# A two-layer decoder on one core: activations grouped by their table, and the end of a running maximum taken in single chunks

## The chip, the core and the metric

The kernel runs on one core of a Trainium2 chip. TensorE (PE in the profile) multiplies matrices, VectorE (DVE), ScalarE (ACT) and GpSimd (POOL) work element by element, and SyncE (SP) issues the transfers. Each engine takes its own instructions in order. The metric is device time in microseconds; lower is better. All data is float32.

## The reference, cut to what matters

The input is 32 sequences of 56 tokens with 128 features, and for each sequence a context of 1500 rows of 128 features. Six blocks follow one another, each added to its input and layer-normalised:

```python
x = _layernorm(x + _L0_attn_ref(x, ...), axis=-1)               # windowed self-attention, 16 heads
x = _layernorm(x + _L0_xattn_ref(ctx_1024, ctx_1024, x, ...))   # one-head attention to the context
x = _layernorm(x + _L0_ffn_ref(x, w_up, w_down, ...))           # 8 experts of 512 units, gelu, top 2 of a softmax router
x = _layernorm(x + _L1_attn_ref(x, ...))                        # recurrent mixer
x = _layernorm(x + _L1_xattn_ref(x, ctx_1024, ...))             # 16 heads of 64 attend to the context
x = _layernorm(x + _L1_ffn_ref(x, ...))                         # shared expert and 8 experts of 256 units, top 2
```

The change touches the third block (layer 0's experts, and the two weights of the chosen experts, which are a softmax over the two largest router logits) and the fifth (layer 1's attention to the context: scores, softmax over 1500 rows, and the weighted sum).

## The kernel before, in words

**Layer 1's attention** (`attention`, L1041) is the backbone. The projections of query and key are folded into one 128x128 matrix for each head, so a sequence has 16 x 56 = 896 query columns. They are cut into two blocks, 512 and 384 columns wide; 32 sequences give 64 blocks. For a block, 12 matmuls make the scores `s` of 12 chunks of 125 context rows (through 3 banks of the pool `p_s`); ScalarE copies each chunk to SBUF (L1065); VectorE keeps a running maximum `m`, two chunks at a time, after chunks 3, 5, 7, 9 and 11 (L1068), and at the end folds its two halves into one (L1076). TensorE then transposes `m` (`maxima`, tile `t<-ident,m`), VectorE reduces it to the negative maximum of each query, and TensorE spreads that back (`spread`). Only then, in a second pass over the scores, VectorE adds the negative maximum (L1150) and ScalarE takes the exponential (L1153), three chunks at a time, in four parts (`probabilities`). The first of these parts run between the value matmuls of the block before, the rest (`tail`) in the score phase of the block after. The value matmuls of a block (`values`, 12 for each tile of 128 queries, tile `v`) come one block later, between the scores of the next block and those of the one after: so TensorE has 12 value matmuls between a block's last scores and the transposes of its maximum. The results are transposed into `qo` by `outputs` (L1173, tile `t<-ident,ao`), called at chunk 9 of a later score phase.

**Everything else** is filler: generators that the attention loop advances between its own pieces. `pre(g)` runs layer 0 and the mixer for a group of four sequences (`self_attention`, `cross_attention_0`, `experts_0`, `recurrent_mixer`, `queries_1`), `post(k)` runs layer 1's output projection and experts. A `Thread` holds a generator; `until(th, us)` steps it while its TensorE time, counted by the planner's own estimate, is under what is due. Each `yield` gives a delay that the planner lets pass before the next step. When the attention reaches a group whose `pre` isn't through, `finish` runs the rest at once, with little beside it. The first two groups run before the attention begins: a `leader` and a `follower`, stepped in turn. The framework that builds the program then orders the instructions once more by priority, readiness and free buffers, so the program's order is not exactly the order of the calls.

**`experts_0`** (L703) makes the router's logits, picks two experts (`top2`), and computes the two weights `p1`, `p2` with an exponential on ScalarE (L723), an addition, a reciprocal and a product on VectorE, and from them `wmix` (`mix`). Then, for each of 8 experts, four units of 128: a matmul into a bank of the pool `p_f` (two banks, tag `f`, shared by all filler) and a gelu on ScalarE (L740), with a `yield 0` after each; then the down-projection of the expert before (`down`) and its weighted addition to `acc` (L757). Behind the first expert's gelus, TensorE transposes `wmix` and VectorE copies it to `wT` (L751), from which the experts' biases are added (`bdn`). The weights of the next expert are issued on SP's queue at the start of each expert.

**Tables.** ScalarE needs the right activation table for a function. The builder puts a load (`ACT_TABLE_LOAD` in the profile, `LoadActFuncSet` in the program) wherever the next function isn't in the active table. Gelu and the exponential are in different tables; tanh, copy and identity need no load beside either. In the profile, a load carries the line of the activation behind it.

Of the kernel before, what the change touches and what calls it, by code (L numbers as in the profile page):

```python
# [10 lines left out]
AF = mybir.ActivationFunctionType  # L11
ALU = mybir.AluOpType
AX = mybir.AxisListType

B, S, D, SK = 32, 56, 128, 1500
# [13 lines left out]
PK, CK = 125, 12  # L29
# [40 lines left out]
def decoder_kernel(  # L70
# [35 lines left out]
    def bank(pool, tag):  # L106
        if pool is p_f and place["aside"]:
            pool, tag = p_s, "s"
        return pool.tile([P, 512], F32, tag=tag, name=tag)
# [36 lines left out]
    def mm(ps, lhsT, rhs, start=True, stop=True):  # L146
        nc.tensor.matmul(ps, lhsT=lhsT, rhs=rhs, start=start, stop=stop)  # L147
        n = math.prod(rhs.shape[1:])

        k, m = lhsT.shape[0], math.prod(lhsT.shape[1:])  # L150
        part = 0.5 if k <= 32 else 0.25 if m <= 32 else 0.5 if m <= 64 else 1.0
        clock["pe"] += part * max(4 * n * CYCLE + 0.016, MATMUL_MIN)
# [175 lines left out]
    def linear(lhsT, rhs, n, m=P):  # L328
        ps = bank(p_f, "f")
        mm(ps[:m, :n], lhsT, rhs)  # L330
        return ps[:m, :n]
# [71 lines left out]

    def self_attention(xs):
# [294 lines left out]
    def experts_0(xs):  # L703
        nj, nt = len(xs), len(xs) * TP
        nu = U0 // D

        def weights(e):
            wu = wst.tile([P, U0], F32, tag="w0", name="wu0", bufs=4)
            nc.sync.dma_start(wu, wup0[:, e * U0 : (e + 1) * U0])
            wd = wst.tile([P, U0], F32, tag="w0", name="wd0", bufs=4)  # L710
            nc.sync.dma_start(wd, wdn0[:, e * U0 : (e + 1) * U0])
            return wu, wd

        ws = weights(0)
        xT = to_features(xs, "xT")
        yield HOP
        lg = tiny.tile([TP, nj, E], F32, tag="lg", name="lg", bufs=2)
        nc.vector.tensor_copy(lg, router(xT, C_R0, nj))
        picks = top2(lg)
        p1 = tiny.tile([TP, nj], F32, tag="p1", name="p1", bufs=2)  # L720
        p2 = tiny.tile([TP, nj], F32, tag="p2", name="p2", bufs=2)
        nc.vector.tensor_tensor(p2, picks[1][0], picks[0][0], ALU.subtract)
        nc.scalar.activation(p2, p2, AF.Exp)  # L723
        nc.vector.tensor_scalar_add(p1, p2, 1.0)
        nc.vector.reciprocal(p1, p1)
        nc.vector.tensor_tensor(p2, p2, p1, ALU.mult)
        w = mix(picks, (p1, p2))
        yield 0
        acc = []
        hT = None  # L730
        for e in range(E + 1):
            last = (ws, hT)
            if e < E:
                if e > 0:
                    ws = nxt
                if e + 1 < E:
                    nxt = weights(e + 1)
                hT = hidden_tile()[:, :, :nt]
                for u in range(nu):
                    nc.scalar.activation(  # L740
                        hT[:, u, :], linear(ws[0][:, u * D : (u + 1) * D], xT, nt), AF.Gelu,
                        bias=vec[:, C_BUP + e * nu + u : C_BUP + e * nu + u + 1],
                    )
                    yield 0
            if e == 0:

                wT = work.tile([E, T], F32, tag="wT", name="wT", bufs=1)[:, :nt]
                ps = bank(p_f, "f")
                for j in range(nj):
                    tr(pair(ps[:E], j), w[:, j, :])  # L750
                nc.vector.tensor_copy(wT, ps[:E, :nt])  # L751
                yield HOP
                for j in range(nj):
                    acc.append(plus(linear(pair(wT, j), bdn, D, TP), xs[j], "acc"))
            else:
                for j in range(nj):
                    nc.vector.scalar_tensor_tensor(  # L757
                        acc[j], down(last[1], last[0][1], nu, j),
                        w[:, j, e - 1 : e], acc[j], ALU.mult, ALU.add,
                    )  # L760
                    yield 0
        return acc


# [281 lines left out]
    def attention():  # L1046
        blocks = [(b, q0, n) for b in range(B) for q0, n in BLOCKS]
        prev = None
        old = None
        tail = []  # L1050
        for i in range(len(blocks) + 2):
            cur = None
            if i < len(blocks):
                b, q0, n = blocks[i]
                if q0 == 0:
                    if b % 2 == 0 and any(b // 2 == pairs[0] for pairs in GROUPS):
                        yield ("need", b // 2)
                s = sbig.tile([P, CK, n], F32, tag=f"s{n}", name=f"s{n}")[:PK]
                m = mid.tile([P, 2, 512], F32, tag="m", name="m")[:PK, :, :n]
                qT = qo[(b // 2) % 3][:, b % 2, q0 : q0 + n]  # L1060
                cur = (b, q0, n, s)
                for c in range(CK):
                    ps = bank(p_s, "s")
                    mm(ps[:PK, :n], amT[:, c * PK : (c + 1) * PK], qT)
                    nc.scalar.copy(s[:, c, :], ps[:PK, :n])  # L1065
                    if c % 2 == 1 and c > 1:
                        a = s[:, 0:2, :] if c == 3 else m
                        nc.vector.tensor_tensor(m, a, s[:, c - 1 : c + 1, :], ALU.max)  # L1068
                    if c % 2 == 0 and tail:
                        tail.pop(0)()  # L1070
                    if c == 9 and old is not None:
                        outputs(old)
                        old = None
                    if c % 2:
                        yield 0
                nc.vector.tensor_tensor(m[:, 0, :], m[:, 0, :], m[:, 1, :], ALU.max)  # L1076
                if q0 and b + 1 < B:
                    load_attended_T(b + 1)
            elif old is not None:
                outputs(old)  # L1080
                old = None
            for f in tail:
                f()
            tail = []
            os = []
            nt = prev[2] // P if prev else 0
            for t in range(max(nt, 2)):
                if t < nt:
                    po = values(prev, t)
                    for k in range(3):  # L1090
                        next(po)
                        if t == 1 and k == 1 and cur:
                            nb = spread(cur, nm)
                            tail = probabilities(cur, nb)
                            for f in tail[:1]:
                                f()
                            tail = tail[1:]
                        yield 0
                    os.append(next(po))
                elif t == 1 and cur:  # L1100
                    yield 1.0
                    nb = spread(cur, nm)
                    tail = probabilities(cur, nb)
                if t == 0 and cur:
                    if not nt:
                        yield 1.0
                    nm = maxima(cur, m)
                if t >= 2 and tail:
                    tail.pop(0)()
            if prev:  # L1110
                old = (prev, os)
            if cur and cur[1] == 0 and cur[0] + 1 < B:
                load_attended(cur[0] + 1)
            prev = cur
# [20 lines left out]
    def spread(blk, nm):  # L1135

        n = blk[2]
        ps = bank(p_t, "t")
        for t in range(n // P):
            tr(ps[:PK, t * P : (t + 1) * P], nm[:, t : t + 1].to_broadcast([P, PK]))  # L1140
        nb = mid.tile([PK, 512], F32, tag="nb", name="nb")[:, :n]
        nc.scalar.copy(nb, ps[:PK, :n])  # L1142
        return nb
# [39 lines left out]
    class Thread:  # L1183
        def __init__(self, gen, aside=None):
            self.gen, self.spent, self.at, self.over = gen, 0.0, 0.0, False
            self.aside = aside

        def step(self):
            t0 = clock["pe"]
            place["aside"] = self.aside  # L1190
            try:
                lat = next(self.gen)
            except StopIteration:
                lat, self.over = 0, True
            place["aside"] = None
            self.spent += clock["pe"] - t0
            self.at = clock["pe"] + (lat or 0)
            return lat is not None

        def drain(self, *others):  # L1200
# [39 lines left out]

    def until(th, us):
        while not th.over and th.at <= clock["pe"] and th.spent < us:
            if not th.step():
                break

# [125 lines left out]
```

## Time and profile before

| | |
|---|---|
| time, median of 3 runs | 2231.57 us (2231.19 to 2233.58) |
| the profiled execution | 2235.22 us, its span 2233.5 us |
| mean granted TensorE clock | 0.988 |
| busy: PE, DVE, ACT, POOL | 2160.7, 1434.5, 1269.0, 139.4 us |
| activation-table loads on ACT | 43 at L740, 34 at L1153, 9 at L723, 1 at L268, each 1283 ns |

Each engine's row gives the time in which it had an instruction running. For TensorE, the end of a matmul is modelled, so 97% busy doesn't mean that it runs at its peak. The waits say whom an engine waited for, and a wait is only worth something if it lies on the way to the end. The granted clock is a share of TensorE's full speed over a stretch of time.

### The profile page before, as it was taken

How to read it: one execution, taken by the hardware profiler on the slowest of the kernel's cores; microseconds unless marked ns; L12 is line 12 of the kernel's file. 1: busy time of each engine (PE TensorE's matmuls, PEld its weight loads, DVE VectorE, ACT ScalarE, POOL GpSimd, SP SyncE). 2: the span in 40 equal slices, each digit the busy share in tenths (PEclk: the TensorE clock that was granted, in tenths of full speed). 3: DMA queues.
4: the chain of work that ended last, by engine and by line, in shares of the span. 5: the costliest groups of instructions: out<-in, count | busy, mean ns of one | idle time of the engine just before them, and what ended most of it. 6: DMA issues, size and time to landing. Idle time of an engine off the chain costs nothing.

```text
span 2233.5 us, 36792 instructions
## 1 busy us (share of the span) xinstructions
PE 2160.7 (97%) x14560; PEld 1709.6 (77%) x14560; DVE 1434.5 (64%) x2926; ACT 1269.0 (57%) x2207; POOL 139.4 (6%) x230
## 2 busy tenths in 40 slices
PE   7899999999999999999999999999999999999997
PEld 5667778678877888777877778777887778778787
DVE  4368554776567656766567665776557766676674
ACT  2555575566655566555665466656565556565551
POOL 2000001100010000100001000110001000000000
PEclk9899999999999999999999999999999999999999
DMA  7621322043211432025311243114330132111221
GB/s 198 173 85 31 111 51 94 17 125 85 93 30 56 117 86 79 22 68 127 94 55 31 77 114 105 48 29 111 92 98 28 56 103 74 51 40 44 66 80 37
DMA packets 164299, 172.16 MB, mean 77 GB/s; under 512 B 9464, under 2 KB 136864, under 8 KB 164000
## 3 DMA queue, kind: packets, MB, share of 16 engines
q1 hardware_dynamic: 164128, 169.82, 27.0%
q8 instruction: 115, 1.88, 0.4%
q14 instruction: 56, 0.46, 0.1%
HBM read 144.29 MB, written 25.49 MB: 76 GB/s over the span
## 4 chain that ended last, share of the span: by engine, by line
PE 80%; DVE 9%; ACT 5%; POOL 2%; DMA 2%; issue 1%; SPq 0%; POOLq 0%; ACTq 0%; DVEq 0%
PE f L147 29%; PE s L147 24%; PE v L147 21%; PE f L156 4%; PE t L156 3%; DVE s L1150 3%; ACT s L1153 2%; POOL rs L360 2%; DVE m L1068 2%; DMA memT<-big 1%; DVE st L351 1%; DMA wu<-in_wup_dram 0%; ACT nb L1142 0%; ACT s L1065 0%; DVE y L365 0%
## 5 line engine op out<-in xcount | busy, mean ns | idle before, releaser
L147 PE MATMUL v<-amN,s 125*128 125x129 f32 x5376 | 702.2, 276 | 2.6 <-ACT s L1153 1.8
L147 PEld LDWEIGHTS v<-amN,s 125*128 125x128 f32 x5376 | 662.4, 192 | 39.6 <-issue 22.3
L147 PE MATMUL s<-qo,amT 128*125 128x512 f32 (+1 forms) x1536 | 652.3, 544 | 2.4 <-ACT s L1065 2.2
L1065 ACT COPY s<-s 125x512 f32<-125x512 f32 (+1 forms) x768 | 399.2, 537 | 211.0 <-PE s L147 206.4
L1150 DVE TENSOR_TENSOR s<-s,nb 125x1536 f32<-125x1536 f32 (+1 forms) x256 | 393.2, 1549 | 63.2 <-ACT nb L1142 62.8
L147 PEld LDWEIGHTS s<-qo,amT 128*125 128x125 f32 x1536 | 264.4, 188 | 162.0 <-issue 93.3
L1153 ACT ACTIVATE s<-s 125x1536 f32<-125x1536 f32 (+1 forms) x256 | 339.1, 1328 | 85.5 <-DVE s L1150 79.3
L1068 DVE TENSOR_TENSOR m<-m,s 125x1024 f32<-125x1024 f32 (+1 forms) x256 | 278.5, 1088 | 78.8 <-ACT s L1065 75.3
L360 POOL TENSOR_TENSOR rs<-rs,mhalf 112x1 f32<-112x1 f32 x126 | 81.7, 660 | 1721.3 <-DVE rs L359 1465.1
L1170 ACT ACTIVATE ao<-v,rz 128x128 f32<-128x128 f32 x224 | 80.9, 364 | 152.9 <-DVE rz L1168 152.5
L740 ACT ACTIVATE hT<-f,vec 128x224 f32<-128x224 f32 (+1 forms) x256 | 106.3, 437 | 106.2 <-PE f L147 104.1
L147 PE MATMUL f<-xT,wu 128*128 128x224 f32 (+1 forms) x512 | 135.2, 368 | 4.9 <-DMA wu<-in_wup_dram 3.1
L147 PEld LDWEIGHTS f<-wd,hT 128*112 128x112 f32 x960 | 115.3, 180 | 15.5 <-ACT hT L740 4.5
L147 PE MATMUL f<-wd,hT 128*112 128x128 f32 x960 | 125.2, 279 | 1.2 <-ACT hT L740 1.2
L147 PE MATMUL f<-pxT,w 128*128 128x224 f32 (+1 forms) x576 | 118.0, 344 | 2.0 <-DVE th L923 0.7
L147 PEld LDWEIGHTS f<-pxT,w 128*128 128x128 f32 x576 | 98.5, 194 | 17.8 <-DVE th L923 3.7
L147 PEld LDWEIGHTS f<-xT,wu 128*128 128x128 f32 x512 | 86.9, 199 | 32.8 <-ACT hT L740 10.4
L1068 DVE TENSOR_TENSOR m<-s 125x1024 f32<-125x1024 f32 x64 | 69.5, 1086 | 55.0 <-ACT s L1065 54.7
L1142 ACT COPY nb<-t 125x512 f32<-125x512 f32 x64 | 34.0, 531 | 113.5 <-PE t L156 113.2
L757 DVE SCALAR_TENSOR_TENSOR acc<-f,wmix,acc 112x128 f32<-112x128 f32 x120 | 41.5, 348 | 85.0 <-PE f L147 85.0
L147 PE MATMUL f<-w,h 128*112 128x128 f32 x512 | 79.9, 279 | 1.9 <-DVE th L923 1.9
L147 PEld LDWEIGHTS f<-w,h 128*112 128x112 f32 x512 | 66.7, 177 | 17.7 <-issue 4.5
(291 smaller groups left out, 2366.1 us busy)
## 6 DMA issues: line engine op xcount, KB each, us to landing
amT<-memT SPq DMA_DIRECT2D x32, 750.0 KB
amN<-in_mem_dram SPq DMA_DIRECT2D x34, 672.0 KB
memT<-big SPq DMA_DIRECT2D x30, 750.0 KB
cxN<-in_mem_dram SPq DMA_DIRECT2D x30, 672.0 KB
wu<-in_wup_dram SPq DMA_DIRECT2D x72, 256.0 KB
wd<-in_wdn_dram SPq DMA_DIRECT2D x72, 256.0 KB
w<-in_gate_dram SPq DMA_DIRECT2D x72, 128.0 KB
w<-in_up_dram SPq DMA_DIRECT2D x72, 128.0 KB
```

What stands on the lines that cost most here:

```text
L147: nc.tensor.matmul(ps, lhsT=lhsT, rhs=rhs, start=start, stop=stop)
L156: nc.tensor.transpose(ps, in_, ident[:k, :k])
L351: nc.vector.bn_stats(st, r)
L360: nc.gpsimd.tensor_tensor(rs, rs, mhalf[:TP], ALU.pow)
L740: nc.scalar.activation(hT[:, u, :], linear(ws[0][:, u * D : (u + 1) * D], xT, nt), AF.Gelu, bias=vec[:, C_BUP + e * nu + u : C_BUP + e * n ...
L757: nc.vector.scalar_tensor_tensor(acc[j], down(last[1], last[0][1], nu, j), w[:, j, e - 1 : e], acc[j], ALU.mult, ALU.add,)
L1065: nc.scalar.copy(s[:, c, :], ps[:PK, :n])
L1068: nc.vector.tensor_tensor(m, a, s[:, c - 1 : c + 1, :], ALU.max)
L1142: nc.scalar.copy(nb, ps[:PK, :n])
L1150: nc.vector.tensor_tensor(c, c, nb.unsqueeze(1).to_broadcast([PK, 3, n]), ALU.add)
L1153: nc.scalar.activation(c, c, AF.Exp)
L1170: nc.scalar.activation(o, po[:, :D], AF.Copy, scale=rz)
```

## The change

Four things are done.

- In `experts_0`, gelus come in pairs: two units' matmuls go into the two halves of one bank, and two gelus read it. In front of each pair the generator yields a marked delay, `Gelu(0)`. A flag `table["gelu"]` is cleared when the attention begins a block's exponentials and set again when its `tail` is empty, in the next block's score phase. While the flag is clear, `until` holds a thread that stands before a pair of gelus, unless the thread is within 5 us of what is due to it, or past it.
- The router's two weights are made with tanh in place of the exponential: `0.5 + 0.5 tanh(d/2)` and `0.5 - 0.5 tanh(d/2)`, one ScalarE and two VectorE instructions. The transposition of `wmix` and the biases move from behind expert 0's gelus to behind expert 1's. The `yield 0` of the down-projections stands ahead of each instead of behind it.
- The running maximum: the chunks 3, 5, 7 and 9 still go two at a time; right after chunk 9's, the two halves are folded into one; then chunks 10 and 11 are taken singly, each as soon as it is copied. The fold at the end is gone.
- `outputs` is called at chunk 5 instead of chunk 9.

```diff
+    class Gelu(float):
+        pass
+    table = {"gelu": True}
...
-        nc.scalar.activation(p2, p2, AF.Exp)
-        nc.vector.tensor_scalar_add(p1, p2, 1.0)
-        nc.vector.reciprocal(p1, p1)
-        nc.vector.tensor_tensor(p2, p2, p1, ALU.mult)
+        nc.scalar.activation(p2, p2, AF.Tanh, scale=0.5)
+        nc.vector.tensor_scalar(p1, p2, -0.5, 0.5, ALU.mult, ALU.add)
+        nc.vector.tensor_scalar(p2, p2, 0.5, 0.5, ALU.mult, ALU.add)
         w = mix(picks, (p1, p2))
-        yield 0
...
-                for u in range(nu):
-                    nc.scalar.activation(
-                        hT[:, u, :], linear(ws[0][:, u * D : (u + 1) * D], xT, nt), AF.Gelu,
-                        bias=vec[:, C_BUP + e * nu + u : C_BUP + e * nu + u + 1],
-                    )
-                    yield 0
-            if e == 0:
+                for u0 in range(0, nu, 2):
+                    yield Gelu(0)
+                    ps = bank(p_f, "f")
+                    for k in range(2):
+                        u = u0 + k
+                        mm(ps[:, k * nt : (k + 1) * nt], ws[0][:, u * D : (u + 1) * D], xT)
+                    for k in range(2):
+                        c = C_BUP + e * nu + u0 + k
+                        nc.scalar.activation(
+                            hT[:, u0 + k, :], ps[:, k * nt : (k + 1) * nt], AF.Gelu,
+                            bias=vec[:, c : c + 1],
+                        )
+            if e == 1:
+                yield 0
...
-            else:
+            if e > 0:
                 for j in range(nj):
+                    yield 0
                     nc.vector.scalar_tensor_tensor(
                         acc[j], down(last[1], last[0][1], nu, j),
                         w[:, j, e - 1 : e], acc[j], ALU.mult, ALU.add,
                     )
-                    yield 0
...
-                    if c % 2 == 1 and c > 1:
+                    if c % 2 == 1 and 1 < c < CK - 2:
                         a = s[:, 0:2, :] if c == 3 else m
                         nc.vector.tensor_tensor(m, a, s[:, c - 1 : c + 1, :], ALU.max)
+                        if c == CK - 3:
+                            nc.vector.tensor_tensor(m[:, 0, :], m[:, 0, :], m[:, 1, :], ALU.max)
+                    elif c >= CK - 2:
+                        nc.vector.tensor_tensor(m[:, 0, :], m[:, 0, :], s[:, c, :], ALU.max)
                     if c % 2 == 0 and tail:
                         tail.pop(0)()
-                    if c == 9 and old is not None:
+                    if not tail:
+                        table["gelu"] = True
+                    if c == 5 and old is not None:
                         outputs(old)
                         old = None
...
-                nc.vector.tensor_tensor(m[:, 0, :], m[:, 0, :], m[:, 1, :], ALU.max)
...
                         if t == 1 and k == 1 and cur:
+                            table["gelu"] = False
                             nb = spread(cur, nm)
...
     def until(th, us):
         while not th.over and th.at <= clock["pe"] and th.spent < us:
+            if th.gelu and not table["gelu"] and th.spent > us - 5.0:
+                break
             if not th.step():
                 break
```

`Thread.step` sets `self.gelu` when the delay that it was given is a `Gelu`.

## The prediction

> **What bounds the kernel now.** I read the profile from the whole to the wait: the busy shares, the chain that ended last, the groups of the engines that the change touches, TensorE's waits, and stretches around its longest ones. From the page:
>
> ```profile
> span 2233.5 us, 36792 instructions
> PE 2160.7 (97%) x14560; PEld 1709.6 (77%) x14560; DVE 1434.5 (64%) x2926; ACT 1269.0 (57%) x2207; POOL 139.4 (6%) x230
> PE 80%; DVE 9%; ACT 5%; POOL 2%; DMA 2%; issue 1%; SPq 0%; POOLq 0%; ACTq 0%; DVEq 0%
> ```
>
> TensorE is the bound, and the change takes no matmul away. So what can be gained is only time in which TensorE waits, or runs at a lower clock because it waited. The second view is TensorE's waits, longest first:
>
> ```profile
> PE f L156 <- DVE h L365: 7.5, 10, 1.5
> PE t L156 <- DVE rz L1168: 4.5, 5, 1.8
> ...
> PE t L156 <- DVE m L1076: 4.1, 4, 2.1
> ...
> PE f L147 <- DMA wu<-in_wup_dram: 3.1, 1, 3.1
> ...
> PE f L156 <- DVE wmix L683: 2.3, 1, 2.3
> ...
> PE s L147 <- ACT s L1065: 2.2, 6, 1.0
> PE f L147 <- ACT hT L740: 2.2, 5, 1.0
> PE v L147 <- ACT s L1153: 1.8, 2, 1.4
> PE s L156 <- ACT s L622: 1.6, 1, 1.6
> ```
>
> Both waits of `t L156` for `rz` and `m` are the transposes of the running maximum: `rz` is only the VectorE instruction that happened to stand beside the end. They are 9.0 us together. All waits for ScalarE (`hT`, `s`) are a few us. The third view is the groups of ScalarE and, with shapes apart, VectorE that the change alters:
>
> ```profile
> L740 ACT ACT_TABLE_LOAD x43 | 55.2, 1283 | 2.1 <-PE f L147 1.4
> L1153 ACT ACT_TABLE_LOAD x34 | 43.6, 1283 | 0.6
> L723 ACT ACT_TABLE_LOAD x9 | 11.5, 1283 | 0.2
> ```
>
> ```profile
> L1068 DVE TENSOR_TENSOR m<-m,s 125x1024 f32<-125x1024 f32 x128 | 156.4, 1222 | 48.3 <-ACT s L1065 47.4
> L1068 DVE TENSOR_TENSOR m<-m,s 125x768 f32<-125x768 f32 x128 | 122.1, 954 | 30.4 <-ACT s L1065 27.9
> L1076 DVE TENSOR_TENSOR m<-m 125x512 f32<-125x512 f32 x32 | 22.7, 710 | 0.5
> L1076 DVE TENSOR_TENSOR m<-m 125x384 f32<-125x384 f32 x32 | 18.0, 562 | 0.5
> ```
>
> Last, the stretches around two of the longest waits, with the granted clock (PEclk) of each:
>
> ```profile
> core 0: us, PE busy (x), PEclk, DMA share, GB/s
> 300.00:319.80 19.80, 17.41 (x123) 1.00 0.23 44
> 319.80:326.60 6.80, 6.33 (x23) 0.50 0.15 28
> 613.00:616.80 3.80, 1.72 (x16) 1.00 0.00 0
> 616.80:620.20 3.40, 3.40 (x18) 0.50 0.00 0
> 74.10:87.80 13.70, 12.82 (x48) 0.50 0.32 95
> ```
>
> The clock is the number after the bracket. Right behind a wait of 2.3 us (for `wmix`, to 319.7) and one of 2.1 us (for `m`, 613.7 to 615.8) it is 0.50 for 6.8 and 3.4 us: a wait costs its length and half of such a stretch.
>
> **The change, part by part.**
>
> *Router and `wmix`.* In the timeline of 313 to 321 us, ScalarE loads a table (1.28 us) for the router's exponential at 317.08, the exponential ends at 318.58, VectorE finishes `wmix` at 319.6, and TensorE, idle since 317.4, transposes it at 319.74; then it waits again for `wT`, 0.5 us. The change takes the load away and puts the transposition behind another expert: in the built program four more up-projections and over four more value matmuls stand between router and transposition in this group, 4 x 0.53 us (118.9 us busy for 224 of that shape) and 4 x 0.26 (702.2 for 2688), 3.2 us, more than the 2.3. What is late next is nothing: the first down-projection wants expert 0's gelus, done by then. I take both waits as gone, 2.8 us, and the low clock behind them, 6.8 / 2 = 3.4: **-6.2 us**, bounds 0 and -6.2. Eight other routers cost no such wait, so they give nothing.
>
> The Trainium skill ("TensorE: Matmul & The Clock Gate", section "Part 1: The HAM clock gate") lets the clock fall only after an idle window of about 3.4 us, longer than either wait here. By it the stretches of 0.50 would not belong to these waits and would stay, and the sum would be 4.3 us smaller; the two rows, each directly behind its wait, speak for the link, and I go by them.
>
> *Running maximum.* After the last chunk's copy, before: one wide and one fold, 1222 + 710 = 1.93 us in a 512 block, 954 + 562 = 1.52 in a 384 block. After: one single, priced as the fold, 0.71 and 0.56. So the chain is 1.22 or 0.95 us shorter where VectorE is waiting for chunks. Where it is behind already, what remains from chunk 9 on is longer: one wide and three singles, 1222 + 2130 = 3.35, against two wides and a fold, 3.15 us: +0.20 (384: 2.64 against 2.47, +0.17). The timeline shows both kinds: at 1682 us VectorE idles before the wide of chunk 11; at 1152 and 1971 us (waits of 1.8 and 1.4) the wides run back to back. The waits that can go are 9.0 us, the short ones wholly, the long ones hardly: half, **-4.5**, and half of the 1.7 us behind 613, **-0.9**. Bounds: all of it, -10.7, or 10 such waits longer by 0.20, +2. On VectorE's queue the change adds (2 x 0.710 - 1.222) x 32 + (2 x 0.562 - 0.954) x 32 = 11.8 us, and takes some 1.5 off for nine routers; the cover is its own idle third (799 us), 0.
>
> *`outputs` earlier.* No instruction more. The 4 or 3 transposes and the copy of 0.69 or 0.55 us (`qo`, L1178) pass chunks 6 to 9. The copy leaves the end of the score phase, where VectorE is late, which helps the line above; but VectorE is in order, and where `ao` isn't ready at chunk 5 the maxima stand behind the copy. From the score phase's start to chunk 5 there are still six scores, 4.5 us at 0.75 (289.6 us busy for 384 of 384 columns). **0**, bounds -1 and +2.
>
> *Tables.* The built program has 45 loads for 87: 22 before gelus, 22 before the exponentials, none at the router. 42 x 1.283 = 53.9 us less on ScalarE, which is idle 964 us. What TensorE waited for behind such loads after 135 us is at most `hT`, scores and exponentials of the waits shown, 6.2 us; some of it isn't behind a load: **-2**, bounds 0 and -6.2.
>
> *Before the attention* (0 to 135 us) latencies are bare. A load at 70.85 and one at 73.05 surround the leader's exponential, `ao` of the follower (L622) waits behind the first, and TensorE 1.6 us for it; then come 0.50 for 13.7 us. The wait goes: -1.6; a second pair of loads (85.11, 86.62) sits before a 0.4 us wait for `hT`. But expert weights are late here (3.1 us for `wu`), and a faster leader meets them sooner, so I take **-2.5**; bounds -1.6 - 6.9 = -8.5, and one more such wait, +3.1.
>
> *Gate and pairs.* The same matmuls and gelus; a pair fills a bank for two gelus (2 x 0.44) instead of one. `experts_1` takes both `f` banks at once and can stand behind it; held gelus hold back the down-projections, and SP's queue stands behind `wd` (`L711` waits on PE 178.9 us already, with loads of the context behind it). In the built program the pairs mostly stand four matmuls together, 4 x 0.53 us of TensorE against 4 x 0.44 of ScalarE, which keeps up. **0**, bounds -2 and +6.
>
> Sum: -6.2 - 4.5 - 0.9 + 0 - 2 - 2.5 + 0 = -16.1. The profiled execution took 2235.2 us; that gives 2219.1 there. It was 3.65 above the median shown, so 2215.5 for the median; **2216**.
>
> **Rivals.**
>
> *A. The waits go, the low clocks stay or come elsewhere.* The sum loses 3.4 + 0.9, and the starting phase gives nothing: 16.1 - 6.8 = 9.3 off, **2222**. For it: stretches of 0.50 also lie at 384.7, behind a run of short waits that the change leaves. Against: the two rows. This is what the skill's rule of the clock gate comes to.
>
> *B. VectorE is behind at every long wait, and the new order makes as many waits as it removes.* Then only the router's 2.8 us stay, less the 2 us of the backlogged maxima: **2231**. For it: the waits over 1.4 us all have VectorE working up to the end. Against: the copy of `qo` goes from there.
>
> *C. Slower: the gate makes `pre` late.* If gelus are held, the stages behind them are pressed together, and `finish` runs them bare. The price is seen in group 2, which is finished so: between 355 and 390 us TensorE waits 2.3 for `h`, 1.0 for `hT`, 0.6 for `xT`, and the clock is 0.50 for 3.4 us: 5.6 us. It ends slower by over 0.2% (4.5 us) from (16.1 + 4.5) / 5.6 = four of the other six groups on: **2238**. Against it: in both built programs the queries that end a group stand in blocks 15, 23, 31, 39, 47 and 55.
>
> *D. ScalarE's time counts after all*, since late copies feed late maxima: half of the 53.9 us on top of the other terms, **2191**. The Trainium skill ("ScalarE: Activation LUTs", "What ACT_TABLE_LOAD costs") gives about 2.66 us for a switch, drain included, 112 us in all; here the next activation starts 10 ns after the 1283. Against D: TensorE's waits for ScalarE are far too short.
>
> **How the numbers follow.** The forecast has 0.60, with 2208 to 2224 as its own range; A 0.14, B 0.13, C 0.08, D 0.05. What a measurement can tell from no change is about 0.2%, 4.5 us: faster is below 2227.1. The forecast, A and D are faster, 0.79; B the same, 0.13; C slower, 0.08. The range goes from 2203 (the favourable bounds of the maximum and of the starting phase: 6 + 6 below) to 2233, which takes in B; it leaves out C and D.
>
> **What would show it.** Right: 45 loads; no wait for `wmix` and no 0.50 near 320 us; waits of `t L156` below half of 9.0 us; PE busy about as before, the span about 16 shorter. Wrong: waits of `t L156` as long as before, with wides and singles back to back (B); long waits for `h` just before the queries of a group (C); scores waiting for `amT`, or `f` for `th` or `hT` (the gate); a starting phase that ends later than 135 us. The prediction fails if TensorE's waits are not additive, that is, if a wait that goes only lets it meet the next one sooner.

## The result and the profile after

The changed kernel takes 2212.53 us (median of 5 runs, 2210.03 to 2217.40) against 2232.33 (5 runs, 2231.19 to 2233.93): a ratio of 0.9903, 95% interval 0.9891 to 0.9915, 0.97% faster. 2216 was forecast, with a range of 2203 to 2233. The profiled execution took 2217.40 us, the longest of the five, with a span of 2215.7; against that of before (2235.22) it is 17.8 us shorter, where the working of the prediction had 16.1; the medians are 19.8 us apart. The sum was nearly right. Most of its terms were not, as the rest shows.

From the page of the changed kernel, the span, the busy times and the chain by engine:

```profile
span 2215.7 us, 36884 instructions
PE 2146.1 (97%) x14560; PEld 1706.4 (77%) x14560; DVE 1436.4 (65%) x2981; ACT 1208.6 (55%) x2165; POOL 142.5 (6%) x230
PE 68%; DVE 9%; ACT 3%; POOL 2%; issue 1%; DMA 1%; POOLq 0%; SPq 0%; ACTq 0%; DVEq 0%
```

ScalarE is 60.4 us less busy (54 was worked out) and VectorE 1.9 more (10 was worked out). TensorE has the same 14560 matmul records. The table loads in ScalarE's groups are 22 before gelus, 22 before exponentials and none at the router:

```profile
L753 ACT ACT_TABLE_LOAD x22 | 28.2, 1283 | 0.7 <-PE f L147 0.4
L1174 ACT ACT_TABLE_LOAD x22 | 28.2, 1283 | 0.4
```

TensorE's waits in the changed kernel, longest first:

```profile
PE t L156 <- DVE rz L1189: 7.7, 6, 1.7
PE f L156 <- DVE h L365: 7.0, 14, 0.9
PE f L147 <- DMA wu<-in_wup_dram: 6.4, 4, 3.3
PE t L156 <- DVE m L1087: 4.5, 7, 1.4
...
PE f L156 <- DVE wmix L690: 0.3, 1, 0.3
```

Two things are to be seen. The wait for `wmix` fell from 2.3 to 0.3 us, as forecast. The waits of the maximum's transposes (`t L156` for `rz` and `m`) did not halve: they grew from 9.0 to 12.2 us. And the opening waits longer for expert weights (`wu`, 6.4 for 3.1).

So where did 18 us go? The span is cut at points where TensorE has the same work behind it: the first scores of blocks 0, 7, 12, 16 and 63. The stretches of the kernel before (from:to, length, TensorE busy, number of records, granted clock, share of DMA, GB/s):

```profile
core 0: us, PE busy (x), PEclk, DMA share, GB/s
0.00:134.00 134.00, 108.65 (x761) 0.89 0.64 180
134.00:313.80 179.80, 176.30 (x1203) 1.00 0.23 61
313.80:517.70 203.90, 195.30 (x1332) 0.97 0.29 79
517.70:655.20 137.50, 134.29 (x842) 0.99 0.24 71
655.20:2167.80 1512.60, 1492.43 (x10071) 1.00 0.25 72
2167.80:2233.60 65.80, 53.75 (x362) 0.93 0.14 46
```

And those of the changed kernel:

```profile
core 0: us, PE busy (x), PEclk, DMA share, GB/s
0.00:133.90 133.90, 106.93 (x761) 0.92 0.66 179
133.90:313.70 179.80, 176.26 (x1206) 1.00 0.24 62
313.70:505.60 191.90, 188.32 (x1334) 1.00 0.31 84
505.60:640.00 134.40, 131.88 (x833) 1.00 0.24 70
640.00:2148.00 1508.00, 1487.89 (x10076) 1.00 0.26 72
2148.00:2215.80 67.80, 54.87 (x362) 0.90 0.14 44
```

The third row is the answer. Between block 7 and block 12, 12.0 of the 17.8 us are gone, in a tenth of the span. There the experts of group 2 run, and its mixer and queries are finished, in part bare, before the attention may go on to block 8. The granted clock of that row was 0.97 and is 1.00: two stretches at half clock (319.8 to 326.6 and 384.7 to 388.1, 10.2 us together) don't come any more, which is 5.1 us. TensorE's waits inside it, added up, fell from 8.5 to 3.2 us. Together that is 10.4 of the 12.0. The fourth row gave 3.1 (half of it the 3.4 us at half clock behind 616), the long fifth one 4.6 in 1500, the opening nothing, and the end took 2.0 back. In the fifth row the waits are nearly the same (18.7 us before, 18.3 after). What fell there is TensorE's busy time, by 4.5 us; the section on what is needed comes back to it.

### The profile page after: what moved, and what is told of

Read it like the earlier page. It is cut to its first block, busy times and chain, and to the rows that moved or that the text cites. A ratio compares the mean times of both kernels' runs of the same rounds, so it can differ in the third digit from the quotient of the medians.

```text
span 2215.7 us, 36884 instructions
## 1 busy us (share of the span) xinstructions
PE 2146.1 (97%) x14560; PEld 1706.4 (77%) x14560; DVE 1436.4 (65%) x2981; ACT 1208.6 (55%) x2165; POOL 142.5 (6%) x230
## 4 chain that ended last, share of the span: by engine, by line
PE 68%; DVE 9%; ACT 3%; POOL 2%; issue 1%; DMA 1%; POOLq 0%; SPq 0%; ACTq 0%; DVEq 0%
PE f L147 25%; PE s L147 20%; PE v L147 18%; DVE s L1171 4%; PE f L156 3%; PE t L156 3%; POOL rs L360 2%; DVE m L1083 1%; ACT s L1174 1%; DVE m L1087 1%; ACT nb L1163 0%; ACT s L1078 0%; DVE st L351 0%; DMA memT<-big 0%; DVE m L1085 0%
## 5 line engine op out<-in xcount | busy, mean ns | idle before, releaser
L147 PE MATMUL v<-amN,s 125*128 125x129 f32 x5376 | 695.4, 276 | 0.9 <-ACT s L1174 0.5
L147 PEld LDWEIGHTS v<-amN,s 125*128 125x128 f32 x5376 | 655.5, 191 | 36.1 <-issue 23.5
L147 PE MATMUL s<-qo,amT 128*125 128x512 f32 (+1 forms) x1536 | 648.1, 543 | 1.9 <-ACT s L1078 1.9
L147 PEld LDWEIGHTS s<-qo,amT 128*125 128x125 f32 x1536 | 264.1, 188 | 162.9 <-issue 95.2
L1083 DVE TENSOR_TENSOR m<-m,s 125x1024 f32<-125x1024 f32 (+1 forms) x192 | 208.8, 1088 | 67.6 <-ACT s L1078 65.6
L753 ACT ACTIVATE hT<-f,vec 128x224 f32<-128x224 f32 (+1 forms) x256 | 95.3, 435 | 73.8 <-PE f L147 73.3
L147 PEld LDWEIGHTS f<-wd,hT 128*112 128x112 f32 x960 | 114.7, 180 | 16.7 <-ACT hT L753 7.3
L147 PE MATMUL f<-wd,hT 128*112 128x128 f32 x960 | 124.3, 279 | 1.7 <-ACT hT L753 1.4
L147 PE MATMUL f<-pxT,w 128*128 128x224 f32 (+1 forms) x576 | 118.1, 344 | 3.1 <-DMA w<-in_up_dram 1.4
L147 PE MATMUL f<-xT,wu 128*128 128x224 f32 (+1 forms) x512 | 110.3, 351 | 7.6 <-DMA wu<-in_wup_dram 6.4
L147 PEld LDWEIGHTS f<-pxT,w 128*128 128x128 f32 x576 | 99.0, 194 | 20.1 <-issue 4.2
L147 PEld LDWEIGHTS f<-xT,wu 128*128 128x128 f32 x512 | 90.6, 194 | 24.7 <-issue 13.2
L1087 DVE TENSOR_TENSOR m<-m,s 125x384 f32<-125x384 f32 (+1 forms) x128 | 80.3, 628 | 21.2 <-ACT s L1078 14.9
L147 PE MATMUL f<-w,h 128*112 128x128 f32 x512 | 78.7, 276 | 1.6 <-DVE th L936 1.6
```

The costliest lines, as they stand in the source:

```text
L753: nc.scalar.activation(hT[:, u0 + k, :], ps[:, k * nt : (k + 1) * nt], AF.Gelu, bias=vec[:, c : c + 1],)
L1087: nc.vector.tensor_tensor(m[:, 0, :], m[:, 0, :], s[:, c, :], ALU.max)
```

## The experiments

The prediction's theory shares the gain out over its terms: router, maximum, loads, opening. Against it stand theory P (nearly all at one place, where the attention meets group 2; the first expectations call it F), theory L (the loads, 0.42 us for each of the 42 that are gone) and theory M (the maximum's part gives nothing, since VectorE is behind). Ratios are to the kernel before, run on the same chip.

### The four parts, each alone on the kernel before

Router alone:

```diff
-        nc.scalar.activation(p2, p2, AF.Exp)
...
+        nc.scalar.activation(p2, p2, AF.Tanh, scale=0.5)
+        nc.vector.tensor_scalar(p1, p2, -0.5, 0.5, ALU.mult, ALU.add)
+        nc.vector.tensor_scalar(p2, p2, 0.5, 0.5, ALU.mult, ALU.add)
...
-            if e == 0:
+            if e == 1:
```

> The kernel before with the router's part alone: the two weights by tanh, and the transposition of wmix and the biases behind expert 1's gelus. Theory F (one place: group 2's experts, where TensorE waited 2.3 us for wmix and 0.5 for wT and then ran 6.8 us at half clock): no wait for wmix near 318 us, no stretch of 0.50 there, and 6 to 13 us off, most of the whole gain. Theory L (table loads: the whole gain of 17.8 us in the two profiled executions, spread over 42 loads, 0.42 us each): the built program has 65 loads for 87, so 22 x 0.42 = 9 off, spread over all groups. Both give about the same total; the times at which each block's scores start tell them apart: F has the gain before block 9, L has at most a quarter of it there.

The maximum alone (the edit to the chunk loop as in the change, with `outputs` still at chunk 9):

> The kernel before with the running maximum's part alone: fold after chunk 9, chunks 10 and 11 singly, outputs still at chunk 9. The prediction's term: waits of the transposes of m (t L156 for m and rz) fall from 9.0 us to about 4.5, time 5 us lower. Rival M (the long waits are those where VectorE is behind, and there one wide and three singles are 0.2 us longer than two wides and a fold): the waits stay at 9 to 12 us and the time is within 3 us of the kernel before. Theory L: no load goes, 0 us.

The gelus alone (pairs, `Gelu`, the gate and the yields of the change; the exponential stays, and so does `wmix` behind expert 0):

> The kernel before with the gelus' part alone: pairs in one bank, the gate, the yields ahead of the down-projections; the router keeps its exponential, and the transposition of wmix comes behind expert 0's gelus. Theory L: 55 loads for 87, 32 x 0.42 = 13 us off. Theory F: the wait for wmix stays, or is longer, since the exponential stands between two pairs; 0 to 4 us off.

`outputs` alone:

```diff
-                    if c == 9 and old is not None:
+                    if c == 5 and old is not None:
```

> The kernel before with outputs called at chunk 5 instead of 9, and nothing else. The prediction gave it nothing by itself, -1 to +2 us. Rival M: the copy of qo leaves VectorE's queue where it is late, so the waits of the transposes of m fall by some us and the time with them, up to 4 us. Theory L: 79 loads for 87, since the builder orders the filler anew: 3 us off.

Measured, with the stretches cut as above, in us from the profiles:

| | ratio (95% interval) | loads | opening | blocks 0-6 | 7-11 | 12-15 | 16-62 | end |
|---|---|---|---|---|---|---|---|---|
| before | | 87 | 134.0 | 179.8 | 203.9 | 137.5 | 1512.6 | 65.8 |
| changed kernel | 0.9903 (0.9891-0.9915) | 45 | 133.9 | 179.8 | 191.9 | 134.4 | 1508.0 | 67.8 |
| router | 0.9965 (0.9953-0.9977) | 65 | 133.9 | 180.0 | 197.8 | 135.6 | 1510.0 | 67.0 |
| maximum | 0.9993 (0.9982-1.0004) | 87 | 132.7 | 179.1 | 202.8 | 135.4 | 1513.2 | 65.8 |
| gelus | 0.9925 (0.9908-0.9941) | 55 | 126.1 | 180.2 | 193.5 | 136.7 | 1507.9 | 68.1 |
| outputs | 0.9957 (0.9942-0.9972) | 79 | 133.2 | 180.7 | 193.9 | 134.9 | 1512.9 | 68.4 |

The parts alone would add up to 36 us (0.35 + 0.07 + 0.75 + 0.43%), and together they give 22 (0.97%). They don't add, since three of them gain at the same place: blocks 7 to 11 lose 6.1 us by the router, 10.4 by the gelus and 10.0 by the call of `outputs` alone, which touches neither the router nor `wmix`. Its gain there is as large as that of the gelus, which remove four times the loads (32 against 8), so loads are not the cause: theory L falls. The maximum alone can't be told from no change, and the waits of `t<-ident,m` are 9.5 us with it, for 9.0. The prediction's term for it falls.

All of the three, and the changed kernel, lose the whole 10.2 us at half clock in this stage, 5.1 us of time. They differ in the waits that are left there: 7.5 us with the router alone, 5.2 with the gelus, 4.7 with `outputs` and 3.2 in the changed kernel, for 8.5 before. So the router's 6.1 us are hardly shorter waiting. Its wait for `wmix` is gone, but two waits for exponentials stand in its place (`v L147 <- ACT s`, 2.9 us, the longer one 1.7), and no half clock follows them.

Why `outputs` can do it: a call at another chunk makes the builder order the filler anew, and in that order the transposition of `wmix` of group 2 comes with other work in front of it. In that profile no wait for `wmix` of 0.2 us or more is left between 300 and 400 us, and no stretch of 0.50 there. Not every edit does this: the maximum alone keeps the wait of 2.3 us and both stretches at half clock. The accident belongs to some orders and not to others.

### One thing in one group

```diff
-            if e == 0:
+            if e == (1 if g == 2 else 0):
```

(and the down-projections under `if e > 0`; on the kernel before, with the exponential everywhere.)

> The kernel before with one thing changed in one group: in group 2 alone the transposition of wmix and the biases come behind expert 1's gelus; the exponential stays everywhere. Theory P (one place): the wait of 2.3 us for wmix and the stretch of 0.50 at 319.8 go, and with them 5 to 8 us up to block 12; nothing later: time 5 to 8 us below the kernel before, about 2226. Theory L (loads): 85 for 87, less than 1 us. If the clock's low stretch isn't tied to that wait (rival A of the prediction), the wait goes and a stretch of 0.50 stays between 310 and 330 us: about 2.5 us.

Ratio 0.9975 (0.9965 to 0.9985), 5.6 us: the place by itself is worth a quarter of the whole. Blocks 7 to 11 take 199.6 us for 203.9, blocks 12 to 15 135.9 for 137.5, and the long stretch 1511.8 for 1512.6. The rows around the place:

```profile
core 0: us, PE busy (x), PEclk, DMA share, GB/s
310.00:318.20 8.20, 5.61 (x32) 1.00 0.57 126
318.20:321.60 3.40, 3.10 (x12) 0.50 0.01 4
321.60:380.00 58.40, 55.16 (x377) 1.00 0.23 81
```

and TensorE's waits in that kernel between 300 and 400 us, the longest:

```profile
PE f L147 <- ACT hT L740: 2.7, 2, 2.6
PE v L147 <- ACT s L1153: 1.5, 2, 1.2
```

The wait for `wmix` is gone, and a new one of 2.6 us for a gelu, just behind the exponential's two loads that were kept, stands in its place; a stretch of 0.50 follows it, half as long as before. The load had its part in that: with the tanh (router alone) ScalarE has no load for the router there, and neither this wait nor a low clock is left. Added up, TensorE's waits in blocks 7 to 11 are 7.8 us, for 8.5 before. So 3.4 of the 4.3 us gained there are clock: 3.4 us at half clock for 10.2. The stretch at 384.7 is among those that are gone, though the edit doesn't touch what runs there. Moving the transposition of `wmix` alone didn't bring the 10 to 12 us of the gelus, of `outputs` and of the changed kernel, whose waits in this stage are shorter.

### The changed kernel with one part taken back

The maximum as before (wides to the end, one fold):

> The changed kernel with the running maximum as before (wides to the end, one fold), outputs still at chunk 5, router and gelus as changed. Theory M (the maximum's part gives nothing, since VectorE is behind where TensorE waits long): within 3 us of the changed kernel, 2210 to 2216. The prediction's term: 5 us slower than the changed kernel, about 2217.5.

The gate off:

```diff
-                            table["gelu"] = False
```

> The changed kernel without the gate: the flag is never cleared, so gelus run between exponentials; pairs, router, maximum and outputs as changed. 57 loads for 45. Theory L (a load costs what the whole gain comes to per load, 0.42 us): 12 x 0.42 = 5 us slower than the changed kernel. Theory P (the gain sits where the attention meets group 2, and ScalarE's loads lie beside TensorE's work): within 3 us of the changed kernel, and the gain up to block 12 stays at 10 to 13 us.

The router as before (exponential, `if e == 0`):

> The changed kernel with the router as before: exponential, and the transposition of wmix behind expert 0's gelus; gelus, gate, maximum and outputs as changed. 63 loads for 45. Theory L: 18 x 0.42 = 7.6 us slower than the changed kernel. Theory P: the new order gives the transposition of wmix its cover anyhow, as in the kernels with the gelus' part or the outputs' part alone: no stretch of 0.50 near 320 us, within 4 us of the changed kernel. The prediction's step (the router's part is what removes that wait): the wait of 2.3 us and the low clock come back, 6 us slower.

| | median us | ratio (95% interval) | loads | opening | 7-11 |
|---|---|---|---|---|---|
| changed kernel | 2212.53 | 0.9903 (0.9891-0.9915) | 45 | 133.9 | 191.9 |
| without the maximum | 2212.54 | 0.9913 (0.9897-0.9930) | 45 | 132.4 | 191.9 |
| without the gate | 2211.52 | 0.9908 (0.9893-0.9923) | 57 | 134.1 | 192.0 |
| without the router | 2214.86 | 0.9921 (0.9904-0.9938) | 63 | 127.6 | 194.5 |

None can be told from the changed kernel. Twelve loads more cost nothing that can be told (2211.52 for 2212.53, where theory L asks for 5 us more), so theory L is out. The maximum's part gives nothing here either. Its transposes' waits (`t<-ident,m`) are shorter without it, 9.2 for 12.2 us, but they are 9.2 with the gate off as well, where the new maximum stays. Without the router's part no stretch of 0.50 lies near 320 us, as theory P said: in the new order the place has its cover anyhow. What that kernel loses later it wins in the opening, 6.3 us. That was not expected by any theory, and is taken up below.

### Why the maximum's waits did not shrink

The prediction bounded its term by two cases: VectorE waiting for chunks (the chain gets shorter) and VectorE late (it gets longer by 0.2 us). One experiment takes VectorE's work away without touching the last steps (it leaves chunks 6 and 7 out of the maximum):

```diff
-                    if c % 2 == 1 and c > 1:
+                    if c % 2 == 1 and c > 1 and c != 7:
```

> The kernel before with the wide maximum after chunk 7 left out in every block: chunks 6 and 7 aren't in the running maximum, so VectorE has 1.22 or 0.95 us less to do in each score phase, while the chain behind the last chunk is unchanged (one wide, one fold). Theory M (VectorE's backlog makes the long waits of the transposes of m): those waits (t L156 for rz, m) fall from 8.6 to under 5 us, and the time by 4 to 8 us with the low clock behind the wait at 613. Against it (the length of the last steps makes them): waits stay at 7 to 10 us, time within 3 us.

Ratio 0.9985 (0.9975 to 0.9996), 3.4 us (0.9 to 5.6), and the waits of `t<-ident,m` are 7.4 for 9.0 us: the waits as the second expectation has them, the time between the two. Some of the backlog is the sheer amount of work, but most of the waits stay, and the longest grew (2.5 us at 616, for 2.1). What else is in VectorE's queue is seen in its timeline in the changed kernel, before the longest wait (start, duration, instruction):

```profile
861.23 0.21 DVE L359 TENSOR_SCALAR rs<-mv 112x1 f32<-112x1 f32 x2
862.11 0.35 DVE L365 TENSOR_SCALAR h<-acc,mv,rs 112x128 f32<-112x128 f32 x1 [0.67 <-POOL rs L360]
862.62 0.35 DVE L365 TENSOR_SCALAR y<-acc,mv,rs 112x128 f32<-112x128 f32 x1 [0.17 <-POOL rs L360]
862.88 1.22 DVE L1083 TENSOR_TENSOR m<-m,s 125x1024 f32<-125x1024 f32 x1
864.02 0.28 DVE L784 SCALAR_TENSOR_TENSOR res<-y,row 112x128 f32<-112x128 f32 x1
864.22 0.68 DVE L1085 TENSOR_TENSOR m<-m 125x512 f32<-125x512 f32 x1
865.01 1.49 DVE L1087 TENSOR_TENSOR m<-m,s 125x512 f32<-125x512 f32 x2
```

A group's experts have just ended, and their layer norm stands in the score phase: VectorE idles 0.84 us for GpSimd's power (`rs`), and the wide of chunk 9 starts at 862.88. The last chunk's copy ended at 862.85, so all four steps of the new order still lie ahead, 3.4 us, while the value matmuls that cover them end at 864.90. Waits of this kind end at 601.6, 866.6, 1135.0 and 1400.8 us, one for each group (1.3, 1.7, 1.3 and 1.3 us); before, they end at 615.8, 883.3, 1152.3 and 1416.7 (2.1, 1.3, 1.8 and 0.6 us). This reading fits all four, but no run took the layer norm away, so it is seen and not tested. And it doesn't explain the growth: the four are 5.6 us together and were 5.8. What grew are the others. Apart from one of 1.4 us that both kernels have, there were four short ones with 1.5 us, and now there are eight with 5.1, up to 1.1 us each. At 305.5 (0.9 us) and 2161.2 (1.1 us), fold and singles run back to back without a layer norm in between.

The last attempt moves the transposes, and the spread behind them, instead:

```diff
-                if t == 0 and cur:
-                    if not nt:
-                        yield 1.0
-                    nm = maxima(cur, m)
+                if t == 0 and cur and not nt:
+                    yield 1.0
+                    nm = maxima(cur, m)
...
+                        if t == 1 and k == 0 and cur:
+                            nm = maxima(cur, m)
-                        if t == 1 and k == 1 and cur:
+                        if t == 1 and k == 2 and cur:
```

> The changed kernel with the maximum's transposes moved behind four more value matmuls (16 instead of 12 after the last scores, 0.9 us of TensorE's work), and the spread and first exponentials moved behind four more as well. If the waits of t L156 (12.2 us in 13 waits of 0.2 to 1.7 in the changed kernel's profile) are a matter of cover in front of a late VectorE, 0.9 us more takes 8 to 10 us of them off, and the time falls by 5 to 10 us to 2203 to 2208, unless the later exponentials hold up the value matmuls of the next block: then waits of v for ScalarE appear, and the time stays near 2212.

The group of these transposes in the changed kernel (count, busy, mean ns, idle before them and for whom):

```profile
L156 PE MATMUL t<-ident,m 125*128 125x125 f32 x224 | 36.1, 274 | 12.2 <-DVE rz L1189 7.7 <-DVE m L1087 4.5
```

and with the transposes four value matmuls later:

```profile
L156 PE MATMUL t<-ident,m 125*128 125x125 f32 x224 | 36.3, 274 | 5.0 <-DVE m L1087 2.3 <-DVE rz L1190 2.3
```

7.2 us of waits are gone, and the time isn't better: 2215.58 us, ratio 0.9917 (0.9901 to 0.9934). Between the scores of blocks 16 and 63 it gains 2.6 us only (1505.4 for 1508.0); there 10.2 us run at half clock, for 3.4 in the changed kernel, which takes back 3.4. Other waits are longer (`h` 8.0 for 7.0 over the span, `xT` 2.8 for 1.2), and blocks 7 to 11 take 196.0 us for 191.9, with waits of 6.3 for 3.2. The waits were real and the cover removed them, but a wait removed here was mostly not a microsecond gained.

### The opening

```diff
-            if e == 1:
+            if e == (0 if nj == 1 else 1):
                 yield 0
```

> The changed kernel, but in the two groups that run before the attention (one pair each) the transposition of wmix and the biases stay behind expert 0's gelus; the tanh stays. The start of the first scores stood at 133.9 us in the changed kernel and at 126.1 and 127.6 in the two kernels whose router is as before while gelus come in pairs. Theory S (the late transposition holds the first down-projection, and with it the slots of the weights and their loads, where the start waits for weights): first scores at 126 to 129, TensorE's waits for wu fall from 6.4 us to about 4, and the time is 5 to 7 us below the changed kernel, about 2206. Rival (the exponential's loads, not the transposition, or the chance of the low clock): first scores at 132 to 135 and the time as the changed kernel, 2210 to 2214.

2207.39 us, ratio 0.9888 (0.9873 to 0.9903). The median is five below the changed kernel's; the intervals of the two ratios still overlap, so by the time alone this is likely and not shown. In the profile the first scores start at 125.6 us for 133.9. Over all kernels, the opening took 125.6 to 128.6 us in the four with gelus in pairs and the transposition behind expert 0 in these groups, and 130.9 to 134.5 in the ten others. TensorE's waits from 60 to 133 us, in the changed kernel:

```profile
PE f L147 <- DMA wu<-in_wup_dram: 6.4, 4, 3.3
PE f L147 <- ACT hT L753: 1.8, 3, 1.2
PE s L147 <- DMA wu<-in_wup_dram: 1.7, 1, 1.7
```

and with the early transposition:

```profile
PE f L147 <- DMA wu<-in_wup_dram: 3.9, 3, 2.1
PE s L156 <- ACT s L629: 1.5, 1, 1.5
PE s L147 <- DMA wu<-in_wup_dram: 1.4, 2, 1.2
```

The waits for weights fall from 8.1 to 5.3 us, and the granted clock of the opening rises from 0.92 to 0.95: from 60 us to the first scores, 20.5 us run at half clock in the changed kernel and 6.8 here, which is 6.8 us of time. This holds over all kernels: 6.8 to 10.2 us in the four, 13.7 to 27.3 in the ten.

Why the late transposition costs this is not shown. It stands with its delay ahead of the first down-projection, and my theory was that the slots into which the next experts' weights are loaded come free later. But the load of the fourth expert's `wu`, for which TensorE waits 3.3 us, to 82.36, was issued at 76.67 in the changed kernel, and at 77.80 with the early transposition, so not later. And the early kernel of the next section waits longer for weights (6.1 us) than the changed kernel without the maximum (4.5), whose transposition is late and whose opening is 3.8 us longer. The half clock separates the two kinds of kernel, the waits for weights don't.

### What of the change is needed

The kernel just shown, with the gate off and the maximum as before:

> The changed kernel with the early transposition in the two opening groups, and without the gate and without the new running maximum: what is left of the change is the pairs of gelus, the router's tanh and late transposition in the other groups, and outputs at chunk 5. 57 loads for 45. If neither the gate nor the maximum carries anything, as each alone suggested, the time is that of the kernel with the early transposition alone, 2204 to 2210, first scores at 125 to 129 us. If they only cover for one another (either one is enough, both gone is not), 2212 or more.

2208.09 us, ratio 0.9887 (0.9871 to 0.9904), 57 loads, first scores at 128.6: no difference in the time that can be told. Neither the gate nor the maximum is needed, and they don't stand in for one another.

The pairs of gelus carry something by themselves. Between the scores of blocks 16 and 63, TensorE's busy time, with half of any stretch at half clock taken off, is 1485.5 to 1489.7 us in the eight kernels with pairs and 1490.9 to 1494.8 in the six without. The up-projections show it: their group (`f<-xT,wu`, 128x224) keeps TensorE busy for 118.9 us before and 98.8 in the changed kernel, for the same 448 records, two for each matmul. Before, these matmuls mostly come one at a time (112 of 168 times, else two); in the changed kernel two or four follow one another. Part of the 20.1 us is the half clock near 320 us, and part only passes to their neighbours, whose records overlap theirs. What stays is some 4 us of the long stretch, with and without the gate. No run has the pairs without the moved yields, so which of the two it is stays open.

## Why the prediction was right, and where not

*Right: what bounds the kernel.* TensorE is the bound, it has the same matmuls, and the largest part of the gain is waits and low clock: in blocks 7 to 11, 5.3 and 5.1 of 12.0 us. In the long stretch it is neither: some 4 us are TensorE's busy time.

*Router and `wmix`, -6.2: the place was right, the size was luck, the cause too narrow.* Alone it gave 6.1 us in that stage and 7.8 in all. But the prediction had 2.8 us of waits and 3.4 of clock, and the run had 1.0 of waits and 5.1 of clock: the exponentials' waits came in place of the one for `wmix`, and the half clock at 384.7, which the prediction left alone, went too. And I took the wait for something that only the router's part could remove. Three parts remove it, each alone, since each makes a new order; and 4 to 6 us more go there in the other kernels, with the finish of group 2 among them, whose waits and low clock (5.6 us by the prediction's own rival C) I had priced and not counted as a possible gain.

*Running maximum, -5.4: wrong.* (The 9.0 us are the idle time of the whole group; the two rows shown with it come to 8.6.) The waits rose from 9.0 to 12.2 us, and neither adding nor removing this part could be told in the time (0.9993; 2212.54 for 2212.53). The step that failed is "the short ones wholly, the long ones hardly: half". The long ones indeed hardly changed (5.8 and 5.6 us for those behind a group's experts), but the short ones did not go: they rose from 1.5 to 5.1 us. Rival B had it right that the new order makes as many waits as it removes. The low clock behind 613, which the prediction tied to the wait there, is gone in the changed kernel and with this part alone, where that wait is 1.0 us. But it is gone as well with the router alone and with the edit in group 2 alone, where the wait is still 2.1 us.

*Tables, -2: no gain found.* 12 loads more or less: 2211.52 for 2212.53. The 53.9 us left ScalarE, and no gain can be put down to them. Rival D (2191) falls, and with it an account by the number of loads.

*Opening, -2.5: 0.1.* What I missed is that the late transposition itself costs the opening something: 6 to 8 us lay on the other side of this edit, most of it half clock, and the prediction had it only as a bound of +3.1 for one more wait for weights.

*Gate and pairs, 0: the gate yes, the pairs no.* Some 4 us of TensorE's busy time went with the pairs. The step that failed is "the same matmuls and gelus": the same matmuls, two or four in a row, kept TensorE busy for less.

*`outputs`, 0: alone 9.6 us.* I counted what it moves past, and not that the builder orders everything anew.

*Rival A (the low clock isn't tied to the waits): no.* Near 320 us the clock was low behind a wait of 2.3 us, low again for half the time behind one of 2.6 us, and not low where the waits there were 1.7 us and shorter. But a wait doesn't bring the low clock each time, as the 2.1 us above show; the last section has more on that. Where the Trainium skill ("TensorE: Matmul & The Clock Gate", section "Part 1: The HAM clock gate") has the clock fall after an idle window of about 3.4 us, these shorter waits were enough. *Rival C:* the finishes didn't get worse (waits for `h` 7.0 us, for 7.5), and group 2's got better.

So the sum was close because errors cancel, which is luck: about 5 us for the maximum and 5 for loads and opening that never came, against some 6 more at group 2, and 3.1 and 4.6 in the two stretches behind it, less 2.0 at the end.

## What to carry to other kernels

When a scheduler orders the instructions, every edit is also a new order: before an edit is credited with the end of a wait, try another edit that can't have anything to do with it. Cut two traces at points of equal work before reading any wait list; here the cut put two thirds of the gain in a tenth of the span. And ask which part of a bundle loses: taking the late transposition out of the opening made the opening 8.3 us shorter and the median 5 us lower, while the gate, the maximum and twelve table loads could not be told at all.

## What the runs showed of the hardware that was not expected

The low clock comes in pieces of one length: 3.4, 6.8, 10.2, 13.7, 17.1 and 20.5 us in these profiles (the last piece of a profile is cut at its end), and each is 0.50. A wait of 2.1 to 2.6 us was enough for one, and so were four waits of 0.3 to 0.6 us within 4 us (at 890 to 894 us of the changed kernel, then 0.50 from 895.0 to 898.4). A short wait can so cost more than twice its length: 2.3 us near 318, and 3.4 for the 6.8 at half clock behind it.

But a wait of the same length can also cost nothing more. The transposes' wait of 2.1 us at 613.7 to 615.8 before has half clock behind it, and the same wait at 607.5 to 609.6 with the router alone has none. The pieces lie on a fixed grid: in the changed kernel they start at 82.6, 96.2, 106.5, 895.0, 2185.2 and 2212.5 us, which are 4, 3, 231, 378 and 8 steps of 3.413 us apart. Counted by the cells of that grid in all 14 profiles, from 134 to 2170 us and from full clock, half clock followed each of the 13 cells in which TensorE was busy for less than 46%, 6 of the 64 between 46 and 66%, and none of the 8252 above. Before, the cell of that wait (613.44 to 616.85) has 1.33 us of work, 39%; with the router alone the wait is spread over two cells, and the emptier one (605.71 to 609.12) has 1.80 us, 53%. So whether a short wait costs clock depends here on how it falls to the grid, which an edit far ahead of it can shift.
